# Beta added by GpSimd in the first-head passes, hop 1's first splits in the first group's normalization, and step 0's keys spread over twice as many pieces

## The chip, the core and the metric

The kernel runs on one core of a Trainium2 chip. The metric is the device time of one execution in microseconds (us); lower is better. The engines are called as in the profile: PE is TensorE (PEld its weight loads), DVE is VectorE, ACT is ScalarE, POOL is GpSimd and SP is SyncE, which only issues DMAs here. Each engine runs its own instructions in order; they meet through semaphores.

## The reference

Two graph layers on 4096 nodes of 256 features, each as x + layer(relu(layernorm(x))). Layer 0 is a graph attention with 4 heads over `adj`; layer 1 mixes two steps of a row-normalized adjacency (a "hop") with two steps of an attention that keeps the smallest set of entries whose weight reaches 0.9.

```python
h = relu(layernorm(x))
x = x + L0(h, adj)          # per head: e = leaky(src + dst), softmax where adj > 0, times h @ W
                            # then layernorm over the 256 outputs, * gamma + beta
h = relu(layernorm(x))
# L1(h, S=adj):
R = S + eye; R = R / R.sum(-1)
Z = 0; Xf = Xa = h
for n in range(2):
    A = top_p_attention(Xa, W1, W2, W3)   # softmax(q k^T), kept up to 0.9, renormalized
    Xf = R @ Xf
    Xa = A @ Xa
    Z = Z + Xf @ U1[n].T + Xa @ U2[n].T
x = x + layernorm(h + Z) * ln_g + ln_b
```

## The kernel before

The 4096 rows are 32 blocks of 128. `X` holds all of them in SBUF: first x, then the sum x + layer 0, then h of layer 1. Apart from scheduling hints, the order of the instructions on each engine is the order in which the code issues them (`manual_schedule`), within one such section. Between sections an engine may take up an instruction of a later section early if nothing holds it back and a buffer is free.

*Layer 0, prologue.* For each block: layer norm, product with W, exponentials, and a split of the values in three bf16 parts. POOL does a share of it: `third_part` (L275) and the copies into `ut` (L276).

*Layer 0, passes.* There are 16 passes k = (group ig of 8 blocks) x (head h), so that h = 0 in passes 0, 4, 8 and 12, the first-head passes. A pass goes over 16 pairs p of source blocks. For each pair, ACT (for two pairs of the pass DVE) makes the sign tile `g` (L366, L364), DVE makes two masks `m` from `g` and the edges `ax` (L372, L373), and PE multiplies (L392: 32 products into eight accumulator banks). Masks are issued two pairs ahead and have four buffers. Between passes `evacuate` takes the eight banks: an ACT copy with a scale (L406) and a DVE operation (L409) each, and in a first-head pass a DVE sum (L408). The next pass's first products need the first bank free.

The rest of a pass's work is put in the list `later`, of which one entry is done after each pair from p = 2 to p = 12: two for the heads, and behind the last head `closing`: four `stats`, eight `close`, four `relu`, 18 entries with the two. So a group's closing begins in the next group's first-head pass and ends one pass later; that of the last group (blocks 24 to 31) runs in hop 1.
- `stats` ends with `steps` on POOL (L141 to L144: an addition, a power, two products), which gives scale and bias.
- `close` of a block: ACT scales into `ob` (L441, two buffers), DVE multiplies with gamma (L442), POOL adds beta to the block's x (L443), DVE adds `ob` to it (L444), SP stores the row (L445), DVE takes the moments (L149, L150).
- After the eighth, `steps` again; `relu` then makes h of two blocks on ACT (L452).

POOL also copies one column of a mask (L485, "now") every sixth pair, to time the stores of edges to `adj_d` (L487) for the hops, and issues the edge loads of the next group.

*Hop 1* (`hops`) computes R @ X before its row scaling, transposed. It has 4 passes of 32 blocks; `order[n]` is the n-th (pass, block). For each n SP loads the edges `ar` (L572, four buffers, or `aru` for every fifth later), the block of X is split in a high and a low part `hl` (`split`: an ACT copy L579 and a DVE subtraction L580; five buffers, four blocks ahead), `own` adds the diagonal to one block in a group of 8 (DVE L589), and PE does eight products 128x512 (L602) into `mm` (a tile of two banks) and `acc`. The generator yields twice a block, 256 "pieces" in all, i = 0 to 255; a pass ends at i = 63, 127, 191. At its end `drained` copies the four accumulators to SBUF (L613, two by ACT and two by DVE, `acc` before `mm`), and the rows are turned and stored in the following pass.

The first 20 blocks (40 pieces) run beside the rest of the closing. From piece 40 on, each piece is followed by one piece of `fills` and one of `picks`, apart from those of block 30 (and for `picks` some more) in every pass:
- `fills` starts with `projections`, step 0's keys: eight groups of four blocks. Each transposes X (L752), copies it out (`xs`, L753), multiplies (L759) into a tile `pm` of the pool `mm`, copies that out (L761), and turns keys and queries into the other half of `pm` (L766), from where ACT and DVE split them into `kT` and `qT` (L768, L769). Then moments (L784), bounds (L806 and small tables), and for three blocks the logits (L707), their exponentials (L890) and four probes on ACT (L897).
- `picks` finds the threshold of those three blocks on DVE: two masked sums of half a row (L952), 18 maxima (L976), six rounds of a top-8 (L983, L985), small operations and two maskings of half a row (L952).

PSUM has two tiles `mm` (two banks each), of which the hop holds one for a whole pass, and two of `tp` and `acc`. What is left of `fills` and `picks` after the last piece is issued before the attention of step 0 starts. Then that step (to 1780 us), hop 2 and step 1 follow, in which the change touches nothing: `projections` has the same yields there, since n = 1.

The few lines that set the pace:

```python
                if 1 < p < PAIRS - 3 and later:
                    later.pop(0)()
...
                if (n == 0 or i > 10) and i // 2 % NB != NB - 2:
                    next(filling, None)
                    if i // 2 % NB < NB - 3 or i % (2 * NB) == 2 * NB - 1:
                        next(picking, None)
```

Of the kernel before, what the change touches and what calls it, by code (L numbers as in the profile page):

```python
# [11 lines left out]
F32 = mybir.dt.float32  # L12
F32R = mybir.dt.float32r
# [9 lines left out]
ALU = mybir.AluOpType  # L23
# [33 lines left out]
def gat_then_top_p_diffusion(  # L57
# [104 lines left out]
    with tc.tile_pool(name="l0", bufs=1) as l0, tc.tile_pool(name="l0s", bufs=2) as l0s, tc.tile_pool(name="l0o", bufs=1) as l0o:  # L162
# [175 lines left out]
        out_rows = {}  # L338
        later = []

        def sources(k):
# [54 lines left out]
        def evacuate(k):  # L396
# [27 lines left out]
            return [three, divided] + (closing(ig) if h == H - 1 else [])  # L424

        def closing(ig):
            o = out_rows[ig]
# [3 lines left out]
            def stats(i0):  # L431
                for i in range(i0, i0 + 2):
                    moments_of(mv[:, i, :], o[:, i, :])
                if i0 == G0 - 2:
                    scales.extend(steps(mv, G0, l0s))

            def close(i):
# [4 lines left out]
                nc.vector.tensor_mul(ob, ob, gamma_r)  # L442
                nc.gpsimd.tensor_tensor(xb, xb, beta_r, ALU.add)  # L443
                nc.vector.tensor_add(xb, xb, ob)  # L444
# [5 lines left out]
            def relu(i0):  # L450
                for b in range(ig * G0 + i0, ig * G0 + i0 + 2):
                    nc.scalar.activation(X[:, b, :], X[:, b, :], AF.Relu, scale=x_rs[:, b:b + 1], bias=x_nmr[:, b:b + 1])  # L452
            return [lambda i=i: stats(i) for i in range(0, G0, 2)] + [lambda i=i: close(i) for i in range(G0)] \
                + [lambda i=i: relu(i) for i in range(0, G0, 2)]
# [51 lines left out]
        with tc.manual_schedule(engines=every):  # L506
# [20 lines left out]
            for n, (k, p) in enumerate(todo):  # L527
# [10 lines left out]
                if n in rest:  # L538
                    rest[n]()
                if 1 < p < PAIRS - 3 and later:  # L540
                    later.pop(0)()
# [4 lines left out]
        ps1 = ctx.enter_context(tc.tile_pool(name="ps1b", bufs=2, space=PSUM))  # L546
        PASSES = NB // G0
        S = SimpleNamespace(spare=None)

        order = [(p, j) for p in range(PASSES) for j in range(NB)]  # L550

        def hop_of(hop):
            return SimpleNamespace(hop=hop, src={}, ar={}, hl={}, acc=None, begun=0, parted=0, owned=0)

        def source(A, n):
            if n in A.src or n >= len(order):
                return
            if A.hop == 0:
                A.src[n] = X[:, order[n][1], :]
            else:  # L560
                A.src[n] = S.rows.tile([P, D], F32, name="x1", bufs=3) if n % 5 < 3 else S.rows.tile([P, D], F32, name="xa")
                nc.sync.dma_start(A.src[n], xf_d[order[n][1]])

        def edge(A, n):
# [8 lines left out]
            A.ar[n] = ar  # L573

        def split(A, n):
            while A.parted < min(n, len(order)):
                src = A.src[A.parted]
                hl = rp.tile([P, 2, D], F32R, name="hl", bufs=5)
                nc.scalar.copy(hl[:, 0, :], src)  # L579
                nc.vector.tensor_tensor(hl[:, 1, :], src, hl[:, 0, :].bitcast(F32), ALU.subtract)  # L580
                A.hl[A.parted] = hl
                A.parted += 1

# [80 lines left out]

        first_hop = hops(hop_of(0))
        with tc.manual_schedule(engines=every | {ET.SP}):
# [50 lines left out]
    def waits(n):  # L717
        for i in range(n):
            yield

    def projections(cur, n, G):
# [25 lines left out]
        for g in range(NB // 4):  # L747
            xs = l1e.tile([P, 3, 4, P], F32, name="xs", tag="e1")
            for k in range(KC):
# [3 lines left out]
                nc.scalar.copy(xs[:, k], pt)  # L753
            yield from waits(1 + n)
            carried(xs, g, 0)
# [7 lines left out]
            carried(xs, g, 1)  # L763
            yield from waits(n)
            for i in range(4):
# [9 lines left out]
            carried(xs, g, 2)  # L775
            yield from waits(n)
            carried(xs, g, 3)
# [668 lines left out]
```

## Time and profile before

| | us |
|---|---|
| three runs | 2898.01, 2899.59, 2899.8 |
| median | 2899.59 |
| the profiled execution | 2899.5 |
| its span, first to last instruction | 2897.7 |
| mean granted clock of PE | 0.989 |

By stage, from the busy times of the profile's stretches:

| stretch (us from the start) | length | PE busy | DVE | ACT | POOL |
|---|---|---|---|---|---|
| 0 to 102.18, prologue | 102.2 | 65.6 | 78.4 | 65.8 | 79.2 |
| 102.18 to 810.44, layer 0's passes | 708.3 | 701.0 | 524.2 | 536.0 | 101.0 |
| 810.44 to 905, hop 1, pass 0 | 94.6 | 87.6 | 57.3 | 36.7 | 11.6 |
| 905 to 1010, hop 1 | 105.0 | 100.6 | 32.8 | 52.3 | 8.2 |
| 1010 to 1125, rest of hop 1 | 115.0 | 111.3 | 82.4 | 40.1 | 21.4 |
| 1165 to 1780, attention of step 0 | 615.0 | 614.2 | 540.8 | 489.1 | 196.6 |

How to read the profile: a line of the timeline gives start, length, engine, line of the kernel, operation and tiles, and in brackets the idle time of that engine before it with what released it. A line of waits gives the engine with its line, what it waited for, the sum in us, how often, and the longest. Products of PE overlap: two in flight make 0.39 us each a rate of 0.226.

### The profile page before, as it was taken

Reading aid. Unit: us, or ns where it says so; the run is one execution under the profiler, and the core shown is the slowest. Engines: PE = TensorE matmul, PEld = TensorE weight load, DVE = VectorE, ACT = ScalarE, POOL = GpSimd, SP = SyncE. Lnnn points to the kernel's source line nnn. Section 1 sums busy time; section 2 is a strip of 40 time slices with the busy share of each in tenths; the row PEclk is TensorE's granted clock in tenths of the full one; section 3 lists DMA queues with packets and bytes.
Section 4 is the critical chain, followed back from the end, with each engine's and each line's share of the span. In section 5 each row is a group of like instructions: output and inputs, shape, how many; then the busy total and the mean of one; then the engine's idle time right before and its main releaser. Section 6 shows DMA issues by size and latency. Waiting matters only on the chain. (4 is left out here: it accounts for less than half of the span.)

```text
span 2897.7 us, 51524 instructions
## 1 busy us (share of the span) xinstructions
PE 2814.0 (97%) x18777; PEld 2443.1 (84%) x18777; DVE 2171.2 (75%) x5069; ACT 1914.8 (66%) x3061; POOL 878.6 (30%) x1815
## 2 busy tenths in 40 slices
PE   6899999999999999999999999999999999999998
PEld 4799999999977778888888888767778888888887
DVE  7776877778654374888888889234474999999996
ACT  6786787868733634877788775222626777877782
POOL 6501211112010120233323331000204666666664
PEclk8899999999999999999999999999999999999999
DMA  7969577595454784000000000667992111111110
GB/s 177 217 247 223 187 227 195 211 224 187 177 189 158 238 298 164 20 20 26 20 20 20 26 20 19 231 197 236 313 352 68 31 31 38 34 31 31 39 31 25
DMA packets 190362, 376.48 MB, mean 130 GB/s; under 512 B 18192, under 2 KB 143120, under 8 KB 186000
## 3 DMA queue, kind: packets, MB, share of 16 engines
q1 hardware_dynamic: 146960, 275.12, 28.4%
q0 software_dynamic: 21504, 83.89, 12.2%
q10 hardware_dynamic: 21632, 14.05, 1.5%
q8 instruction: 152, 2.49, 0.3%
q14 instruction: 114, 0.93, 0.1%
HBM read 305.55 MB, written 113.57 MB: 145 GB/s over the span
## 5 line engine op out<-in xcount | busy, mean ns | idle before, releaser
L1075 PE MATMUL acc<-X,eT 128*128 128x256 f32 x4096 | 973.7, 383 | 3.3 <-ACT eT L1069 2.8
L1075 PEld LDWEIGHTS acc<-X,eT 128*128 128x128 f32 x4096 | 739.0, 190 | 111.4 <-ACT eT L1069 31.4
L392 PE MATMUL acc<-ut,m 128*128 128x195 bf16 (+1 forms) x8192 | 701.0, 247 | 8.2 <-DVE st L409 5.6
L392 PEld LDWEIGHTS <-m 128*128 128x128 fp8e4 x8192 | 696.4, 97 | 13.2 <-DVE st L409 4.7
L366 ACT ACTIVATE g<-sr,d_big 128x1024 uint8<-128x1024 f32 x444 | 467.7, 1139 | 2.6 <-DVE m L372 2.6
L890 ACT ACTIVATE e<-mm,nm 128x1024 f32<-128x1024 f32 x256 | 286.1, 1118 | 205.5 <-PE mm L707 204.1
L1069 ACT COPY eT<-tp 128x512 f32<-128x512 f32 x512 | 296.4, 580 | 89.7 <-PE tp L1067 89.6
L602 PE MATMUL mm<-ar,hl 128*128 128x512 f32 x844 | 341.8, 408 | 9.2 <-DMA ar<-adj_d 3.6
L976 DVE MAX8 cand<-big 128x8 f32<-128x228 f32 (+1 forms) x1152 | 348.3, 380 | 0.0
L958 DVE SCALAR_TENSOR_TENSOR big<-e,c 128x4096 f32<-128x4096 f32 x58 | 261.9, 4515 | 98.1 <-POOL c L943 58.8
L602 PE MATMUL acc<-ar,hl 128*128 128x512 f32 x844 | 328.3, 392 | 2.2 <-DVE ar L589 2.1
L914 POOL TENSOR_TENSOR sums<-sums 128x2 f32<-128x2 f32 x64 | 12.7, 198 | 1037.8 <-ACT void L897 1037.8
L1067 PE MATMUL tp<-ident,e 128*128 128x128 f32 x2048 | 306.1, 272 | 0.8 <-DVE e L1001 0.8
L1067 PEld LDWEIGHTS tp<-ident,e 128*128 128x128 f32 x2048 | 255.0, 140 | 60.4 <-PE acc L1085 1.2
L372 DVE TENSOR_TENSOR m<-g,ax 128x512 uint32<-128x512 uint32 x256 | 182.3, 712 | 115.5 <-PE acc L392 96.3
L897 ACT ACTIVATE void<-e,c1x 128x2048 int8<-128x2048 f32 x128 | 257.4, 2011 | 3.3 <-issue 2.5
L1001 DVE SCALAR_TENSOR_TENSOR e<-e,found 128x4096 f32<-128x4096 f32 x58 | 259.1, 4468 | 0.0
L897 ACT ACTIVATE void<-e,c 128x2048 int8<-128x2048 f32 x128 | 257.4, 2011 | 0.0
L707 PE MATMUL mm<-kT,qT 128*128 128x512 f32 x512 | 198.3, 468 | 3.6 <-ACT e L890 2.2
L602 PEld LDWEIGHTS mm<-ar,hl 128*128 128x128 f32 x844 | 158.8, 188 | 49.5 <-issue 9.2
L373 DVE TENSOR_TENSOR m<-m,ax 128x512 uint32<-128x512 uint32 x256 | 177.7, 694 | 26.0 <-DVE m L372 0.9
L602 PEld LDWEIGHTS acc<-ar,hl 128*128 128x128 f32 x844 | 158.8, 188 | 38.8 <-issue 4.1
(303 smaller groups left out, 3538.9 us busy)
## 6 DMA issues: line engine op xcount, KB each, us to landing
ar<-adj_d SPq DMA_DIRECT2D x211, 512.0 KB, 4.6
adj_d<-ax POOLq DMA_DIRECT2D x32, 2048.0 KB, 7.0
ut<-uv_d SPq DMA_DIRECT2D x60, 784.0 KB, 5.7
aru<-adj_d SPq DMA_DIRECT2D x45, 512.0 KB, 4.5
ax<-in_adj_t_dram POOLq DMA_DIRECT2D x32, 512.0 KB, 16.1
x<-xf_d SPq DMA_DIRECT2D x78, 128.0 KB, 4.9
xf<-xft_d SPq DMA_DIRECT2D x64, 128.0 KB, 2.2
sr<-s_d SPq DMA_DIRECT2D x15, 512.0 KB, 4.9
```

Of the source, the lines that this page charges most:

```text
L366: nc.scalar.activation(g[:, c, :], shared[k].sr, AF.Relu, scale=BIG, bias=d_big[:, h, j:j + 1])
L392: nc.tensor.matmul(shared[k].acc[i][:, t, :cols], m[t][:, c, ts(i, P)], shared[k].ut[j // QUARTER][:, j % QUARTER, t, :cols], start=(j == ...
L602: nc.tensor.matmul(A.acc[c][s], A.hl[m][:, t, ts(s, P)], A.ar[m][:, ts(c, 512)], start=(j == 0 and t == 0), stop=(j == NB - 1 and t == 1))
L707: nc.tensor.matmul(pm[:, h, :], q[t], kT[:, ds(h * (N // 2) + c * 512, 512)], start=(t == 0), stop=(t == 1))
L890: nc.scalar.activation(ev[:, :, c, :], r.pm[c], AF.Exp, bias=r.nm, accum_out=r.sums[:, c // 2, c % 2:c % 2 + 1])
L897: nc.scalar.activation(void, r.e[:, ts(h, N // 2)], (AF.Relu, AF.Sign)[i], bias=r.c1, scale=-1.0, accum_out=r.sums[:, h, 2 + i:3 + i])
L958: nc.vector.scalar_tensor_tensor(big, r.e, r.c3, r.e, ALU.is_le, ALU.mult, accum_out=r.low3)
L976: nc.vector.max(cand[:, s, :], big[:, edges[s]:edges[s + 1]])
L1001: nc.vector.scalar_tensor_tensor(r.e, r.e, r.t, r.e, ALU.is_ge, ALU.mult, accum_out=kept)
L1067: nc.tensor.transpose(pt[:, i, :], r.e[:, ts(4 * g + i, P)], ident)
L1069: nc.scalar.copy(eT, pt)
L1075: nc.tensor.matmul(r.acc[:, 0, :], eT[:, i, :], cur[:, j, :], start=(j == 0), stop=(j == NB - 1))
```

## The change

Three parts:
1. The POOL addition of beta leaves `close`. A list `lifted` of the 32 blocks is worked off in the first-head passes, one block after each pair from p = 3 to p = 14 while there are any, directly on `X`. So passes 0 and 4 take 12 each and pass 8 the last 8.
2. `source` and `split` move up in the code, unchanged, with `order`, `hop_of`, `S` and `PASSES`. The hop's state `hop1` is made before the passes, and the first group's `relu` of blocks 0 to 4 is followed by the blocks' split; `hops(hop1)` then finds five splits done.
3. In `projections`, at n = 0, a group takes six pieces for three: two in place of one ahead of the product, one more ahead of the turning of keys, one more at the end. At n = 1 the number stays.

```diff
@@ -337,6 +337,7 @@
         later = []
+        lifted = list(range(NB))
@@ -423,6 +424,34 @@
+        PASSES = NB // G0
+        S = SimpleNamespace(spare=None)
+
+        order = [(p, j) for p in range(PASSES) for j in range(NB)]
+
+        def hop_of(hop):
+            return SimpleNamespace(hop=hop, src={}, ar={}, hl={}, acc=None, begun=0, parted=0, owned=0)
+
+        def source(A, n):
+            if n in A.src or n >= len(order):
+                return
+            if A.hop == 0:
+                A.src[n] = X[:, order[n][1], :]
...
+        def split(A, n):
+            while A.parted < min(n, len(order)):
+                src = A.src[A.parted]
+                hl = rp.tile([P, 2, D], F32R, name="hl", bufs=5)
+                nc.scalar.copy(hl[:, 0, :], src)
+                nc.vector.tensor_tensor(hl[:, 1, :], src, hl[:, 0, :].bitcast(F32), ALU.subtract)
+                A.hl[A.parted] = hl
+                A.parted += 1
+
+        hop1 = hop_of(0)
+
         def closing(ig):
@@ -440,7 +469,6 @@
                 nc.vector.tensor_mul(ob, ob, gamma_r)
-                nc.gpsimd.tensor_tensor(xb, xb, beta_r, ALU.add)
                 nc.vector.tensor_add(xb, xb, ob)
@@ -450,6 +478,10 @@
                     nc.scalar.activation(X[:, b, :], X[:, b, :], AF.Relu, scale=x_rs[:, b:b + 1], bias=x_nmr[:, b:b + 1])
+                if ig == 0 and i0 < LOOK + 1:
+                    for b in range(i0, min(i0 + 2, LOOK + 1)):
+                        source(hop1, b)
+                        split(hop1, b + 1)
@@ -537,6 +569,9 @@
                     rest[n]()
+                if k % H == 0 and 2 < p < PAIRS - 1 and lifted:
+                    b = lifted.pop(0)
+                    nc.gpsimd.tensor_tensor(X[:, b, :], X[:, b, :], beta_r, ALU.add)
                 if 1 < p < PAIRS - 3 and later:
                     later.pop(0)()
...
-        first_hop = hops(hop_of(0))
+        first_hop = hops(hop1)
@@ -751,7 +760,7 @@
                 nc.scalar.copy(xs[:, k], pt)
-            yield from waits(1 + n)
+            yield from waits(2)
             carried(xs, g, 0)
@@ -761,7 +770,7 @@
             carried(xs, g, 1)
-            yield from waits(n)
+            yield
             for i in range(4):
@@ -773,7 +782,7 @@
             carried(xs, g, 2)
-            yield from waits(n)
+            yield
             carried(xs, g, 3)
             if n > 0:
                 yield
```

## The prediction

> **What bounds the kernel now.** I read the page first, then TensorE's waits, then the timeline of the engines around each gap.
>
> ```profile
> PE 2814.0 (97%) x18777; PEld 2443.1 (84%) x18777; DVE 2171.2 (75%) x5069; ACT 1914.8 (66%) x3061; POOL 878.6 (30%) x1815
> ```
>
> TensorE is busy 2814.0 of 2897.7 us. The change takes no TensorE work away, so it can only fill gaps: 83.7 us in all, of which the first 102 us (the prologue) hold 36.6, and the stages from 1780 us on, which are not touched, 24.2. Some 23 us of gaps are left to be had. The waits of TensorE that lie in the changed stretch (line, what was waited for: sum, times, longest):
>
> ```profile
> PE acc L392 <- DVE st L409: 5.6, 4, 1.6
> ...
> PE mm L602 <- DMA ar<-adj_d: 3.6, 4, 1.2
> ...
> PE mm L784 <- DVE qT L769: 1.9, 1, 1.9
> PE mm L759 <- DVE stage L613: 1.6, 1, 1.6
> ```
>
> Only four of the fifteen changes of pass in layer 0 cost TensorE anything. Its timeline there (start, length, idle before and releaser):
>
> ```profile
> 323.75 44.17 PE L392 MATMUL acc<-ut,m 128*128 128x195 bf16 x512 [1.33 <-DVE st L409]
> 369.53 50.69 PE L392 MATMUL acc<-ut,m 128*128 128x195 bf16 x594 [1.61 <-DVE st L409]
> ...
> 501.67 174.84 PE L392 MATMUL acc<-ut,m 128*128 128x195 bf16 x2048 [1.32 <-DVE st L409]
> 677.84 27.93 PE L392 MATMUL acc<-ut,m 128*128 128x195 bf16 x321 [1.33 <-DVE st L409]
> ```
>
> A pass has 512 products, so the 2048 from 501.67 on run through passes 9 to 12 with no gap: an evacuation costs nothing unless something delays it. What delays three of the four is in POOL's and DVE's timelines at 320 us (the same at 498 and 674):
>
> ```profile
> 320.52 1.42 POOL L443 TENSOR_TENSOR X<-X,beta_r 128x256 f32<-128x256 f32 x2
> ```
> ```profile
> 320.34 2.15 DVE L372 TENSOR_TENSOR m<-g,ax 128x512 uint32<-128x512 uint32 x1
> ```
>
> Two beta additions had queued on POOL behind the copy L485, which waited for a mask until 319.69; they run just then, and a mask that takes 0.69 us elsewhere takes 2.15, ahead of the evacuation on DVE. The fourth gap is ACT's:
>
> ```profile
> 366.34 1.62 ACT L579 CAST hl<-X 128x256 fp32r<-128x256 f32 x5
> 367.86 2.58 ACT L406 ACTIVATE st<-acc,e_c 128x195 f32<-128x195 f32 x8
> ```
>
> So hop 1's first five splits are not at the start of the hop: they already run in pass 5, just ahead of its evacuation. At hop 1's start, POOL and SP:
>
> ```profile
> 826.92 6.61 POOL L443 TENSOR_TENSOR X<-X,beta_r 128x256 f32<-128x256 f32 x8
> ```
> ```profile
> 829.54 0.34 SPq L445 DMA_DIRECT2D x_d<-X  x1
> 829.99 0.42 SPq L572 DMA_DIRECT2D ar<-adj_d  x1
> 832.28 0.34 SPq L445 DMA_DIRECT2D x_d<-X  x1
> 832.73 0.37 SPq L572 DMA_DIRECT2D ar<-adj_d  x1
> ```
>
> Each edge load `ar` queues on SP behind the store of a row that DVE has yet to finish. TensorE waits for `ar` at 833.76 (1.24), 836.63 (0.82) and 839.94 us (1.22). Last, the clock behind the change of pass in hop 1 (PE busy, other engines, granted clock, DMA):
>
> ```profile
> 905.00:906.00 1.00, 1.00 (x7) 1.00 (x7) 0.13 (x1) 0.00 (x0) 0.00 (x0) 0.50 0.06 16
> ```
>
> **What the Trainium skill says.** "SBUF — State Buffer", section "Who interferes with whom": a DVE instruction with two SBUF inputs and a GpSimd instruction that reads SBUF take one port pair in turn, and the loser blocks. The trace agrees (0.69 to 2.15 us beside 1.42 us of additions); in the run of five additions at 302.14 us DVE's two-input operations lose only 0.34 to 0.57 each. "TensorE: Matmul & The Clock Gate", section "What's actually happening": the clock falls to half after an idle window of about 3.4 us. The trace shows half clock from 905 to 908 us, though no single gap was that long: 0.97 and 1.64 us, four matmuls between.
>
> **Part 1, beta.** The 32 additions (0.72 to 0.77 us) leave `close` and go to p = 3 to 14 of passes 0 and 4 and p = 3 to 10 of pass 8. They wait for nothing, so POOL runs them as soon as its queue lets it; behind them stand the steps of the normalization and the stores `adj_d`, at most one addition later in passes 4 and 8, and those stores are read only in hop 1.
> - Changes of pass 8 to 9 and 12 to 13: no addition is left there; 1.32 + 1.33 = 2.65 gained. 4 to 5: the addition of p = 14 still follows L485, one in place of two: half of 1.33, 0.65 (0 to 1.33).
> - A wait of 0.17 for a mask in pass 13 (705.94 us) goes with the 1.0 us that `close` waits for POOL at 339 us (the same in each group).
> - Pass 0: POOL is in the prologue's last copies until 119.8 us, then some ten additions run in a row while DVE catches up. Pass 1 starts at 322.42 - 174.84 = 147.58 us (four passes without a gap), a pair of blocks takes 2.73, so the products of p = 8 and 10 start at 125.7 and 131.2; their masks are ready at 122.9 and 127.9, 2.8 and 3.3 us ahead. Taking turns, ten additions cost DVE ten times 0.34 to 0.72, 3.4 to 7.2 us, by p = 10 or 11: a stall of 0 to 3.9; I take 0.8, turn for turn.
> - Pass 4: POOL runs p = 8 to 13 in a row from 302 us, six where five were. The mask for p = 15 is ready at 319.02 us, its products start at 322.42 - 2.73 = 319.69: a margin of 0.67, of which the sixth takes 0.34 to 0.72. I take 0.3 (0 to 1).
> - Hop 1's start: DVE's five stretched operations lose 0.59, 0.35, 0.54, 0.36 and 0.57, 2.4 us. The stores and the `ar` loads behind them come up to 2.4 us earlier. The first two waits vanish, of the third a part stays, and the DMA share there is already 0.73 to 0.99: 2.3 of the 3.3 gained (0.5 to 3.3).
>
> **Part 2, splits.** Five ACT copies (1.5 us together) and five DVE subtractions (0.42) go from 366 to 345 us, between the `relu`s. ACT is busy without a gap from 343.69 to 367.86, so the move alone doesn't start the evacuation earlier. Two things do: the subtractions are out of DVE's way (it evacuates from 368.9 now), and the `relu`s start 1.0 to 1.5 us earlier, since `close` no longer waits for POOL. TensorE ends pass 5 at 367.92: 1.61 go to about 0.1, gain 1.5 (0.5 to 1.6). SP and POOL get nothing from it.
>
> **Part 3, keys.** Hop 1 yields 256 pieces, two for each block; keys start with piece 40. A group of four blocks takes 3 pieces before and 6 after, so all that follows comes 24 pieces later (21 where skipped pieces make up for it); no instruction is added. Groups 4 to 7 go past the change to pass 1, at piece 64.
> - The short waits inside groups (0.6 for `xs`, 0.2 for `qT`): 0.8 gained, since a further piece of four products (0.9 us) lies in between.
> - Change to pass 1: now 0.97 + 1.64 + 1.90 = 4.5. After it group 3 holds one of the two `mm` buffers over piece 64, so TensorE must wait for the other to drain: two DVE copies of 0.69 and signalling, 1.6. The moments' wait of 1.90 loses a piece of 0.9 and is 1.0. Gain 1.9 (0 to 3).
> - One gap of 1.6 has not dropped the clock elsewhere (1.90 before 912.11 did not). Products of L759 took 3.40 there against 2.31, L602's first 0.77 against 0.47: 1.4 gained (0 to 1.4).
> - Change to pass 2, piece 128: the first exponential of block 1 now falls on it, and its logits wait for the drain: 0.7 lost (0 to 1.5).
> - The three picks end later. By count, block 2's masking (2 x 2.35 us on DVE) falls behind the last piece. DVE is idle there between 1124.4 and 1132.3 us, so it is free; without that cover, 4.9.
> - TensorE lost 3.2 us to DVE and ACT at 1025 to 1036, with the picks. The same work comes 21 pieces later: no change (2 gained to 4 lost).
>
> **Sum.** Gains 2.65 + 0.65 + 0.17 + 2.3 + 1.5 + 0.8 + 1.9 + 1.4 = 11.4. Costs 0.8 + 0.3 + 0.7 = 1.8. Net 9.6, off the profiled execution's 2899.5 us (span 2897.7); that execution stands 0.1 below the median of the runs. Forecast 2890.0.
>
> **Rivals.**
> - *Only the beta part counts.* The change to pass 1 gains nothing and the clock stays low; piece 128 costs 1.5, the picks 1, and the additions of pass 0 stall TensorE for 3. Beta and splits gain 7.3 in the sum, so 7.3 + 0.8 - 1.5 - 1 - 3 - 0.3 = 2.3: 2897.2. For it: the buffer is held by count. Against: the gaps at 904 and 912 are there now, with less time to hide them.
> - *SP's loads are bound by DMA.* Rows and edges together are 640 KB for each block's 1.8 us of products, and the queues was at 349 GB/s at 840 us. Then hop 1's start gives nothing: 2892.3. For it: the share of 0.99; against: the first wait stands behind a late issue, at a share of 0.73.
> - *DVE saturates in the picks; slower.* A pick is 22.6 us of DVE work. In pieces 154 to 255 three picks less the last masking (62.9), 51 splits of 0.42 (21.4), 16 `own` additions of 0.28 (4.5) and two drains (2.7) come to 91.5 us, on 101 pieces of 0.906 (91.5) and some 4 us of logits and turned rows. If the backlog passes the four splits that run ahead (7.2 us), each further 2.35 us masking holds up TensorE as at 1025 us, 3.2 per 16 pieces, and over 101 pieces that is 20: 2890.0 + 20 = 2910. Against it: the same load fitted from 1002 to 1106 us before, with gaps.
>
> **How the numbers follow.** Forecast, a gain over 5.8 us (0.2%, about what a measurement can tell from no change), 0.54, with the start bound by DMA 0.12; beta only 0.22; saturation 0.12. Faster 0.66, same 0.22, slower 0.12. The bounds of the forecast alone, not all at once, reach from 2883 to 2895; with most of the second case, 2883 to 2898.
>
> **What would show it.** Right: no gaps near 499 and 675 us; a mask of at most 1.4 us near 320; ACT's evacuation near 366.5; no waits for `ar` in 826 to 842; one gap of about 1.6 at piece 64 and full clock behind it. Wrong: a wait for masks in 120 to 135 us, half clock after piece 64, waits for `hl` all through passes 2 and 3, or `big` drained late at the hop's end.

## The result and the profile after

| | before | after |
|---|---|---|
| median of six runs each, us | 2898.97 | 2884.53 |
| range, us | 2898.01 to 2902.43 | 2883.23 to 2890.51 |
| the profiled execution: its span, us | 2897.7 | 2881.5 |

The ratio of the times is 0.9952, with an interval of 0.9939 to 0.9965: the changed kernel is 14.4 us faster. The forecast was 9.6 us.

From here on the names of the lines are those of the changed kernel: L393 the products of layer 0 (L392 before), L373 and L374 the masks, L410 the evacuation on DVE, L574 the lifted additions of beta, L448 and L449 the splits, L473 and L590 the stores of rows and the edge loads on SP, L611 the products of the hop (L602 before), L768 those of the keys (L759 before). The row of busy times in the page of the changed kernel:

```profile
PE 2804.6 (97%) x18777; PEld 2442.7 (85%) x18777; DVE 2170.3 (75%) x5069; ACT 1916.2 (67%) x3061; POOL 882.0 (31%) x1815
```

The other engines do the same work as before. TensorE executes the same 18777 instructions and yet is busy 9.4 us less: not only gaps have gone, but also time in which it counted as busy while its products came more slowly. Apart from the clock, the forecast had looked for gaps alone.

TensorE's waits after (line, what was waited for: sum, times, longest):

```profile
PE acc L393 <- DVE m L373: 3.0, 2, 1.9
...
PE acc L393 <- DVE m L374: 1.6, 3, 0.6
PE mm L611 <- ACT ob L470: 1.6, 1, 1.6
PE mm L611 <- DVE stage L622: 1.4, 1, 1.4
...
PE tp L761 <- ACT stage L641: 1.0, 1, 1.0
...
PE mm L793 <- DVE qT L778: 1.0, 1, 1.0
PE mm L611 <- DMA ar<-adj_d: 0.9, 1, 0.9
...
PE acc L393 <- DVE st L410: 0.7, 1, 0.7
```

The evacuation's 5.6 us in four waits are down to 0.7 in one, and the waits for `qT` are 1.0 for 1.9. In return there are waits for masks (1.1 of L374's 1.6, and 1.06 of L373's 3.0; the rest of both lies near 102 us, as before) and one of a new kind, `tp` for `stage`. The waits at the hop's start are not gone: 1.63 us at 832.70, which is listed under `ob` although the hop's products do not read it, and 0.95 for `ar` at 842.97. The kernel before had 3.28 in three. TensorE's timeline in layer 0 shows where (start, length, idle before and releaser):

```profile
323.44 25.58 PE L393 MATMUL acc<-ut,m 128*128 128x195 bf16 x289 [0.71 <-DVE st L410]
349.56 2.81 PE L393 MATMUL acc<-ut,m 128*128 128x195 bf16 x31 [0.54 <-DVE m L374]
353.43 0.26 PE L393 MATMUL acc<-ut,m 128*128 128x195 bf16 x1 [1.06 <-DVE m L373]
354.22 365.97 PE L393 MATMUL acc<-ut,m 128*128 128x195 bf16 x4300 [0.54 <-DVE m L374]
```

The gaps near 499, 675 and 706 us are gone, and so is the one ahead of pass 6 near 369 us. The one ahead of pass 5 is 0.71 for 1.33. Three new ones stand inside pass 5, at 349 to 354 us. DVE's and POOL's timelines around the change from pass 4 to 5:

```profile
319.32 0.68 DVE L373 TENSOR_TENSOR m<-g,ax 128x512 uint32<-128x512 uint32 x1
320.11 0.69 DVE L374 TENSOR_TENSOR m<-m,ax 128x512 uint32<-128x512 uint32 x1
320.72 1.48 DVE L373 TENSOR_TENSOR m<-g,ax 128x512 uint32<-128x512 uint32 x1
```
```profile
302.46 4.98 POOL L574 TENSOR_TENSOR X<-X,beta_r 128x256 f32<-128x256 f32 x6
...
320.90 0.74 POOL L574 TENSOR_TENSOR X<-X,beta_r 128x256 f32<-128x256 f32 x1
```

One late addition makes one mask 1.48 us long, where two made it 2.15. Six additions in a row at 302 us cost TensorE nothing.

**How the stages were measured.** Two numbers can be read to about 0.1 us in every profile. The first is the start of the hop's first product. It has to be corrected for one thing: after the prologue TensorE's clock goes from half to full at a moment that differs by execution, between some 105.7 and 108.7 us, in all kernels alike. The products done from 100 to 112 us, counted in three windows of 4 us (79 to 98 in the executions here; 92 is taken as the norm), show by how much, at about 0.085 us each (the 32 products of a pair take 2.73). The second is the time from the hop's first product to a given piece, four products to a piece. Each row is one execution, the profiled one. In us:

| execution | hop 1 starts, corrected | pieces 0 to 40 | 40 to 255 |
|---|---|---|---|
| before, twice | 810.78, 810.71 | 41.17, 41.42 | 270.40, 270.26 |
| only beta | 805.81 | 39.29 | 268.23 |
| only splits | 812.71 | 42.74 | 267.93 |
| only keys | 810.79 | 42.42 | 261.47 |
| without splits | 805.96 | 39.42 | 261.43 |
| changed kernel, twice | 807.17, 807.25 | 39.54, 38.77 | 260.90, 260.53 |
| keys, four pieces | 807.14 | 40.15 | 263.92 |
| keys late | 807.13 | 38.54 | 265.26 |
| stores by POOL | 807.21 | 37.54 | 261.52 |
| moved | 803.33 | 40.31 | 261.12 |
| all three | 803.33 | 37.65 | 261.16 |
| stepped | 803.30 | 37.35 | 259.78 |

Kernels with the same layer 0 agree within 0.15 us in the first column, which shows that the correction holds. What follows the hop is 1773.0 to 1779.6 us in these executions, without an order by kernel: the totals of single executions scatter by that.

### The profile page after: what moved, and what is told of

It is laid out like the page before. It is cut to its first block, busy times and chain, and to the rows that moved or that the text cites. A ratio compares the mean times of both kernels' runs of the same rounds, so it can differ in the third digit from the quotient of the medians.

```text
span 2881.5 us, 51472 instructions
## 1 busy us (share of the span) xinstructions
PE 2804.6 (97%) x18777; PEld 2442.7 (85%) x18777; DVE 2170.3 (75%) x5069; ACT 1916.2 (67%) x3061; POOL 882.0 (31%) x1815
## 5 line engine op out<-in xcount | busy, mean ns | idle before, releaser
L393 PE MATMUL acc<-ut,m 128*128 128x195 bf16 (+1 forms) x8192 | 701.1, 247 | 5.4 <-DVE m L373 3.0
L393 PEld LDWEIGHTS <-m 128*128 128x128 fp8e4 x8192 | 698.0, 97 | 8.8 <-DVE m L373 4.2
L611 PE MATMUL mm<-ar,hl 128*128 128x512 f32 x844 | 341.2, 407 | 6.5 <-ACT ob L470 1.6
L611 PE MATMUL acc<-ar,hl 128*128 128x512 f32 x844 | 328.4, 392 | 0.2
L373 DVE TENSOR_TENSOR m<-g,ax 128x512 uint32<-128x512 uint32 x256 | 179.9, 703 | 106.7 <-PE acc L393 93.0
L374 DVE TENSOR_TENSOR m<-m,ax 128x512 uint32<-128x512 uint32 x256 | 180.5, 705 | 25.2
L611 PEld LDWEIGHTS mm<-ar,hl 128*128 128x128 f32 x844 | 158.6, 188 | 45.7 <-issue 5.8
L611 PEld LDWEIGHTS acc<-ar,hl 128*128 128x128 f32 x844 | 158.8, 188 | 36.6 <-issue 4.1
```

The costliest lines, as they stand in the source:

```text
L393: nc.tensor.matmul(shared[k].acc[i][:, t, :cols], m[t][:, c, ts(i, P)], shared[k].ut[j // QUARTER][:, j % QUARTER, t, :cols], start=(j == ...
L611: nc.tensor.matmul(A.acc[c][s], A.hl[m][:, t, ts(s, P)], A.ar[m][:, ts(c, 512)], start=(j == 0 and t == 0), stop=(j == NB - 1 and t == 1))
```

## The experiments

The first four take the parts of the change singly, on one chip, with 30 runs of the kernel before beside them (2900.68 us).

**Beta alone.** The kernel before with the list `lifted` and without the addition in `close`:

```diff
-                nc.gpsimd.tensor_tensor(xb, xb, beta_r, ALU.add)
...
+                if k % H == 0 and 2 < p < PAIRS - 1 and lifted:
+                    b = lifted.pop(0)
+                    nc.gpsimd.tensor_tensor(X[:, b, :], X[:, b, :], beta_r, ALU.add)
```

> The kernel before with the first part alone (beta lifted out of the closing). Theory A (from the two traces: the key pieces bring most): three gaps at changes of pass gone or halved, 2.65 + 0.6, the mask wait 0.17, hop 1's start 0.7, together about 4.0 us faster than before. Theory B (the sum on record): 5.8 gained less 1.1 lost, 4.7 faster. Theory C (beta is what counts): 8 or more faster. The change to pass 1 in hop 1 keeps its gaps of about 0.97, 1.64 and 1.90 us and its half clock under A and B.

Measured: 2893.22 us, ratio 0.9978 (0.9970 to 0.9986), 7.5 us faster by the medians, 4.1 to 8.7 by the interval: above theory A, between B and C, and the interval excludes neither of these two. The table has the parts: layer 0 ends 4.9 us earlier, the hop's first 40 pieces take 2.0 less. The gaps at the change to pass 1 stayed as theories A and B had it, but not the half clock, and that is another 1.5 us in pieces 64 to 72 (18.70 for 20.23). Theory A was too low in both of the first terms. In layer 0 the listed gaps shrank by only 3.3 us (5.76 to 2.47). The rest is in how a gap is read. These are the counts of one stretch with a gap of 1.32 us in it, in the kernel before, and then of the same 4 us without a gap in the kernel "moved" below (stretch and its length, then PE's busy time with its products, PEld, DVE, ACT, POOL, clock, DMA share, GB/s):

```profile
500.00:504.00 4.00, 2.68 (x29) 1.82 (x26) 3.90 (x18) 4.00 (x7) 0.00 (x0) 1.00 1.04 410
```
```profile
500.00:504.00 4.00, 4.00 (x49) 3.91 (x47) 3.93 (x8) 4.00 (x6) 0.00 (x0) 1.00 0.72 287
```

20 products are missing, 1.7 us at 0.085, where the gap is listed with 1.32. The timeline shows two reasons. A product is listed with 0.25 us although one starts every 0.085, so the idle time is counted from some 0.17 us too late. And behind the gap TensorE is "busy", but each bank has to wait for its own evacuation: the DVE operations come 0.39 us apart, where the four products of a bank take 0.34. Set against "moved", which has no gaps in layer 0, the kernel before loses 7.4 us there for 5.76 of listed gaps, and the changed kernel 3.9 for 2.85: 1.3 to 1.4 times the idle time.

**Keys alone.** The kernel before with the three waits of `projections` as changed:

```diff
-            yield from waits(1 + n)
+            yield from waits(2)
             carried(xs, g, 0)
...
-            yield from waits(n)
+            yield
...
-            yield from waits(n)
+            yield
```

> The kernel before with the third part alone (six pieces for a group of keys). Theory A: it takes most of the gain, 8 to 10 us faster than before; hop 1's start keeps its three waits for edges (3.3 us), and the four gaps at changes of pass in layer 0 stay. Theory B (the sum on record): 0.8 + 1.9 + 1.4 - 0.7 = 3.4 faster. Theory C: within 1 us of before, or slower.

Measured: 2892.62 us, ratio 0.9970 (0.9960 to 0.9980), 8.1 us faster by the medians; layer 0 is untouched (810.79 us), and the first 40 pieces are not shortened (42.42). Theory A holds, the sum on record does not for this part. Against the two kernels of old pace with full clock (268.23 and 267.93), pieces 40 to 255 take 6.6 us less, against the kernel before, which lost clock, 8.9.

**Splits alone.** The kernel before with the second part only:

```diff
                     nc.scalar.activation(X[:, b, :], X[:, b, :], AF.Relu, scale=x_rs[:, b:b + 1], bias=x_nmr[:, b:b + 1])
+                if ig == 0 and i0 < LOOK + 1:
+                    for b in range(i0, min(i0 + 2, LOOK + 1)):
+                        source(hop1, b)
+                        split(hop1, b + 1)
```

> The kernel before with the second part alone (five splits between the relus of the first group). Theory A: the gap of 1.6 us ahead of pass 6 goes, but waits for masks of about 2 us come up in pass 5 where the splits stand ahead of the signs on ACT: 0 to 1 us slower than before. Theory B (the sum on record): up to 1.5 faster, less whatever POOL's beta additions, which stay in the closing here, hold up.

Measured: 2902.38 us, ratio 1.0007 (0.9999 to 1.0016), 1.7 us slower by the medians, an interval that just takes in no change. Layer 0 ends 2.0 us later. Theory A's direction is confirmed by the profile, the record's sign is wrong.

**Without the splits.** The changed kernel less those four lines:

> The changed kernel without the second part: the splits of blocks 0 to 4 back at the hop's first pieces, beta and keys as changed. Theory A: pass 5 loses its waits for masks (2.1 us) and the gap of 1.6 ahead of pass 6 comes back: 0.5 us faster than the changed kernel, to 0.5 slower. Theory B: 1.5 us slower than the changed kernel, so 13 faster than before rather than 14.4.

Measured: 2884.85 us, ratio 0.9943 (0.9930 to 0.9957); the changed kernel has 0.9952, and the two intervals overlap. By the table layer 0 ends 1.2 to 1.3 us earlier without the splits. Pieces 40 to 255 take 0.5 to 0.9 more, but other kernels that have the splits in the relus lie as high (261.52), so that is scatter. The second part costs layer 0 1.2 us, and no gain stands against it. Beta alone and keys alone together give 15.5 us by the medians, and this kernel, which has both, 15.8: they add.

Why the splits cost is in ACT's timeline in pass 5 of the changed kernel:

```profile
345.94 1.07 ACT L480 ACTIVATE X<-X,x_nmr,x_rs 128x256 f32<-128x256 f32 x2
346.93 0.69 ACT L448 CAST hl<-X 128x256 fp32r<-128x256 f32 x2
347.53 2.18 ACT L367 ACTIVATE g<-sr,d_big 128x1024 uint8<-128x1024 f32 x2
...
351.89 14.65 ACT L367 ACTIVATE g<-sr,d_big 128x1024 uint8<-128x1024 f32 x14
368.30 2.80 ACT L407 ACTIVATE st<-acc,e_c 128x195 f32<-128x195 f32 x8 [1.76 <-PE acc L393]
```

A pair has 2.73 us. Two signs take 2.1 of it, a `relu` of two blocks 1.0, two splits 0.6: 3.7 in all, so ACT falls back by a microsecond with each pair that has all of these, and the signs, masks and products behind it with it. By the time of the evacuation it has caught up and is idle for 1.76 us. The count of products shows what it cost; the changed kernel first, then the kernel "moved" below, which has no splits in this pass:

```profile
340.00:350.00 10.00, 9.36 (x107) 8.74 (x105) 4.17 (x9) 7.75 (x13) 2.07 (x3) 1.00 0.71 259
350.00:360.00 10.00, 8.40 (x97) 8.01 (x96) 8.56 (x16) 10.00 (x13) 0.84 (x2) 1.00 0.14 54
```
```profile
340.00:350.00 10.00, 10.00 (x120) 10.00 (x118) 5.39 (x9) 8.19 (x13) 1.62 (x3) 1.00 0.67 246
350.00:360.00 10.00, 10.00 (x121) 10.00 (x119) 8.63 (x16) 10.00 (x11) 0.84 (x2) 1.00 0.59 229
```

204 products for 241: 37 fewer, 3.1 us, for 2.14 of listed gaps. Against that stands the gap ahead of pass 6 (1.75 listed in the kernel without splits).

The next four ask what the keys' gain is made of, and what bounds the hop's start (before: 2899.83 us).

**The kernel before, once more.**

> The kernel before, unchanged, profiled once more. The first profile shows half clock for 3 us behind the change to pass 1 of hop 1, and that stretch 1.5 us longer than in the two kernels that have only beta or only the splits changed, with gaps of the same lengths there. Theory A (the drop of the clock is the execution's, not the kernel's): full clock there in this execution, pieces 64 to 72 take 18.7 us for 20.2. Theory B (the kernel's gaps bring it): half clock again, 20.2 us.

Measured: 2900.26 us, one run. Pieces 64 to 72 take 20.18 us again, as theory B had it, but the half clock is not where it was. In the second execution the clock stays full behind 0.97 and 1.64 us and falls after the wait of 1.89 that ends at 910.87. Of five executions with such a group of gaps three lost clock, about 1.5 us each; only beta and only splits, with the same three gaps, did not. Of seven that have one gap of 1.4 us in its place and six pieces to a group none did: their pieces 64 to 72 all take 11.07 to 11.09.

What decides is the place of the gaps on a grid of 3.41 us, as the clock column of the profiles shows. Here are the stretches of that length around the changes of the clock, in the first profile of before, in this one, and in only splits (columns as above, the clock third from the end):

```profile
901.25:904.66 3.41, 1.56 (x7) 1.09 (x8) 3.31 (x7) 2.37 (x6) 0.00 (x0) 1.00 0.29 114
904.66:908.07 3.41, 3.41 (x17) 3.31 (x16) 0.83 (x3) 0.00 (x0) 0.00 (x0) 0.50 0.02 5
```
```profile
902.14:905.55 3.41, 1.77 (x12) 1.31 (x11) 3.24 (x7) 1.80 (x5) 0.00 (x0) 1.00 0.14 55
905.55:908.97 3.42, 3.42 (x22) 2.53 (x20) 0.96 (x2) 0.58 (x1) 0.00 (x0) 1.00 0.14 23
908.97:912.38 3.41, 1.52 (x19) 1.42 (x19) 2.70 (x5) 0.89 (x2) 0.00 (x0) 1.00 0.34 131
912.38:915.79 3.41, 3.41 (x21) 2.54 (x20) 0.55 (x2) 0.40 (x1) 0.00 (x0) 0.50 0.34 94
```
```profile
1030.02:1033.44 3.42, 1.65 (x7) 1.04 (x6) 3.25 (x15) 1.30 (x4) 2.84 (x8) 1.00 0.95 336
1033.44:1036.85 3.41, 3.24 (x14) 2.70 (x15) 3.27 (x11) 0.41 (x1) 3.05 (x6) 1.00 0.73 228
```

In each execution all changes of the clock lie whole multiples of 3.413 us apart: in the first profile at 105.94, 904.66 and 908.07 us (234 and 1 steps), in this one at 106.84, 912.38, 915.80, 1031.85 and 1035.26 (236, 1, 34 and 1). Where the grid lies differs by execution. In hop 1 the clock fell behind each stretch of the grid in which TensorE was idle for 1.85 us or more, five in all (1.85 in before, 1.89 and 1.92 in this execution, 2.24 in keys late, 2.58 in four pieces for a group), and behind none with 1.78 or less (only splits, above); each time it was full again one stretch later. So the gaps of 0.97 and 1.64 us together cost clock only where the grid puts enough of them in one stretch, and a single gap of 1.4 is too short for it by this count. Each theory holds half: the kernel's gaps make the loss possible, the execution decides. This execution lost clock a second time, behind a wait of 1.92 us at 1031.25; pieces 40 to 255 are not longer for it (270.26 for 270.40), since a wait of 0.66 that follows in the first execution is missing.

**Four pieces for a group.** Only the piece ahead of the product stays:

```diff
             carried(xs, g, 1)
-            yield
+            yield from waits(n)
...
             carried(xs, g, 2)
-            yield
+            yield from waits(n)
```

> The changed kernel with four pieces for a group of keys in place of six: only the further piece between the transposes and the product stays. Theory A (the distance between a copy and the product that reads it is what pays inside a group): the product of 16 takes some 2.0 us as with six pieces, the turning of keys still comes one piece behind its copy, so half or more of the 3 us of overlap is kept, but the keys now end at piece 72, across the change to pass 1: 0 to 3 us slower than the changed kernel. Theory B (it is only the pace, fewer key instructions for each piece): the gain goes with the number of pieces, a third of 6.7, so 4.5 us slower.

Measured: 2889.03 us, ratio 0.9962 (0.9948 to 0.9976). Pieces 40 to 255 take 263.92, 3.0 to 3.4 more than in the changed kernel's two profiles. That is between the theories, and it is not a matter of pace: one wait alone is longer than the difference. TensorE's, and what ACT had ahead of the split it waited for:

```profile
1019.94 0.47 PE L611 MATMUL mm<-ar,hl 128*128 128x512 f32 x1 [4.16 <-ACT hl L448]
```
```profile
1014.50 2.00 ACT L906 ACTIVATE void<-e,c1x 128x2048 int8<-128x2048 f32 x1
...
1016.79 2.00 ACT L906 ACTIVATE void<-e,c1x 128x2048 int8<-128x2048 f32 x1
```

Two probes with a split between them, in the reach of pieces whose products take 0.9 us each, use up the splits that ran ahead, and the clock falls behind it (0.66 from 1020 to 1025 us), which costs another 1.5 us or so. In the changed kernel the probes fall elsewhere, and the longest wait there is 0.72. Before those probes this kernel has no gap at all from piece 40 to 64 (38.90 us, all of them busy). So in this comparison the place of the later work decides more than the two further pieces of a group.

**Keys late.** The old three pieces for a group, and the 24 pieces that this saves put behind the groups:

```diff
...
+        if n == 0:
+            yield from waits(24)
         moments = rows.tile([2 * DA, DA + 1], F32, name="moments", tag="q_s", bufs=3)
```

> The changed kernel with the old pace of three pieces for a group, and 24 pieces of waiting between the eighth group and the moments, so that all that follows the groups comes where the changed kernel has it. Theory A (distance inside groups): groups lose their overlap again, product of 16 at 2.1 to 2.3 us, and the short waits come back: some 3.9 us slower than the changed kernel, less the 1.4 us wait at piece 64, which no group then meets: 2.5 slower. Theory C (what counts is what comes later: moments away from the change of pass, picks in a free place): as fast as the changed kernel or up to 1.4 faster.

Measured: 2887.80 us, ratio 0.9962 (0.9948 to 0.9976). Pieces 40 to 255 take 265.26, of which 1.5 is lost clock: 263.8. This splits the keys' gain in two, as far as single executions allow. From 268.1 (old pace, full clock: the mean of only beta and only splits) to 263.8 are 4.3 us that come from delay alone: moments, tables and picks that fall later. From 263.8 to 261.2 (the mean of the seven executions with six pieces and no other change to the keys) are 2.6 us from distance inside the groups, net of what the wider groups meet at the change to pass 1. That is the size of theory A, 2.5; theory C does not hold. The keys' products show it (busy us, mean ns, idle before and releasers), in turn before, only beta, this kernel and the changed one:

```profile
L759 PE MATMUL mm<-wkq,xs 128*128 128x128 f32 x128 | 18.6, 299 | 2.5 <-DVE stage L613 1.6 <-ACT xs L753 0.6 <-DVE qT L769 0.2
```
```profile
L762 PE MATMUL mm<-wkq,xs 128*128 128x128 f32 x128 | 17.2, 284 | 2.6 <-DVE stage L616 1.6 <-ACT xs L756 0.6 <-DVE qT L772 0.2
```
```profile
L768 PE MATMUL mm<-wkq,xs 128*128 128x128 f32 x128 | 18.8, 301 | 2.5 <-DVE stage L622 1.6 <-ACT xs L762 0.6
```
```profile
L768 PE MATMUL mm<-wkq,xs 128*128 128x128 f32 x128 | 15.6, 275 | 0.0
```

18.6 and 18.8 hold the lost clock, 17.2 does not. The idle time ahead of these products goes from 2.5 to nothing, and the same 128 products take 1.6 us less besides. The wait of 1.64 for the drain, which theory A had hoped away here, stayed: the eighth group still reaches past piece 64, because the pieces of block 30 carry no keys.

**Stores by POOL.** The changed kernel, with the rows of the last group stored by GpSimd:

```diff
-                nc.sync.dma_start(x1_d[b], xb)
+                (nc.gpsimd if ig == NB // G0 - 1 else nc.sync).dma_start(x1_d[b], xb)
```

> The changed kernel with the last group's stores of rows (x1) issued by GpSimd in place of SyncE, so that no edge load stands behind a store. Theory A (late issue): the waits of 1.63 and 0.95 us in the first 40 pieces go, those pieces take 37.7 us for 39.5. Theory B (the DMAs themselves are the limit there, at a share of 0.95 to 1.0): the waits stay within 0.5 us, 39 to 40 us.

Measured: one run of 2886.53 us; the first 40 pieces take 37.54 us, against 38.5 to 40.3 in the six kernels with beta lifted and the stores on SP. Theory A had said 37.7. The two kernels at the end that have this change as well take 37.65 and 37.35. SP's queue in the changed kernel, then in this one:

```profile
828.50 0.34 SPq L473 DMA_DIRECT2D x_d<-X  x1
828.93 0.38 SPq L590 DMA_DIRECT2D ar<-adj_d  x1
830.28 0.34 SPq L473 DMA_DIRECT2D x_d<-X  x1
830.72 0.72 SPq L590 DMA_DIRECT2D ar<-adj_d  x1
```
```profile
823.64 21.36 SPq L590 DMA_DIRECT2D ar<-adj_d  x12
```

A load no longer stands behind a store that waits for DVE, and each comes as soon as a buffer is free. Both waits of the changed kernel, 1.63 and 0.95 us, are gone, so the one listed under `ob` hung on the loads too. The DMA share was 0.94 to 1.02 in 827 to 843 us in this kernel (350 GB/s on average, 330 in the changed kernel), and yet the waits went. A share near 1 did not mean that the loads set the pace. The stores also go by another queue here; no run separates that from the order of issue.

The last four try what the experiments point to, beside the changed kernel on one chip (before: 2900.21 us).

**The changed kernel, once more.**

> The changed kernel, unchanged, on the same chip as the three that follow, so that they can be set beside it: 14 to 15 us faster than before, no half clock in hop 1, 39 to 40 us for its first 40 pieces.

Measured: 2886.78 us, ratio 0.9954 (0.9940 to 0.9968), 13.4 us faster by the medians, a little under what was expected, and the stages as in its first profile but for 0.8 us at the hop's start.

**Moved.** The splits go to pass 6, one after each of five pairs, and beta stops at p = 13:

```diff
-                if ig == 0 and i0 < LOOK + 1:
-                    for b in range(i0, min(i0 + 2, LOOK + 1)):
-                        source(hop1, b)
-                        split(hop1, b + 1)
...
-                if k % H == 0 and 2 < p < PAIRS - 1 and lifted:
+                if k == H + 2 and 2 < p < LOOK + 4:
+                    source(hop1, p - 3)
+                    split(hop1, p - 2)
+                if k % H == 0 and 2 < p < PAIRS - 2 and lifted:
```

> The changed kernel with the five splits in pass 6 (after the pairs p = 3 to 7, one each) in place of between the relus, and with beta added after p = 3 to 13 only, so that none follows p = 14 of pass 4. Theory A: the waits for masks in pass 5 (0.54 + 1.06 + 0.54 us) go, no gap comes back ahead of pass 6, and the gap of 0.71 ahead of pass 5 goes: 2.9 us faster than the changed kernel. Theory B (ACT and DVE are full in pass 5 whatever is added): the evacuation of pass 5 is late all the same, gain under 1 us.

Measured: 2882.77 us, ratio 0.9935 (0.9921 to 0.9948), 4.0 us faster than the changed kernel by the medians. Layer 0 ends 3.9 us earlier, for an expected 2.9: again the listed gaps (2.85) fall short of what they cost. Theory A holds. From pass 1 to pass 15 TensorE has no gap left; this is its line from 150 to 790 us:

```profile
149.84 640.35 PE L393 MATMUL acc<-ut,m 128*128 128x195 bf16 x7519
```

**All three.** With the last group's stores by POOL as well:

> As the one before, and the last group's stores of rows issued by GpSimd. Theory A: the gains add, 2.9 in layer 0 and 1.4 to 2.0 in hop 1, 4.3 to 4.9 us faster than the changed kernel, so about 19 faster than before. Theory B: what is gained ahead of hop 1 brings its loads closer together and is lost there again, under 3.

Measured: 2880.52 us, ratio 0.9931 (0.9918 to 0.9945), 6.3 us faster than the changed kernel beside it by the medians (4.3 to 4.9 expected) and 19.7 faster than before. The hop starts at 803.33, its first 40 pieces take 37.65: both gains are there in full. With the next one this is the fastest version found, and its interval lies below 0.9954, the ratio of the changed kernel on this chip (the two intervals overlap by 0.0005).

**Stepped.** The product of the fourth group held back past piece 64:

```diff
-            yield from waits(2)
+            yield from waits(7 if n == 0 and g == 3 else 2)
             carried(xs, g, 0)
```

> As the one before, and the product of the fourth group of keys held back by five pieces, past the change to pass 1, so that no group holds an mm buffer over piece 64. Theory A: the wait of 1.38 us for the drain at piece 64 goes, and the later steps move by five pieces at no cost: up to 1.4 us faster than the one before. Theory C: what comes later (moments, logits, picks) meets the change to pass 2 or the hop's end elsewhere, and 1 to 3 us are lost.

Measured: 2880.63 us, ratio 0.9929 (0.9914 to 0.9944): the same time as the one before. The wait of 1.38 us is gone, and pieces 40 to 255 take 1.4 us less, as theory A had it, but one execution's remainder is longer by more than that (1778.67 for 1775.77), and the median does not show a gain. Whether it is one stays open.

## Where the forecast held and where it failed

**Beta in layer 0** (recorded: 2.65 + 0.65 + 0.17 gained, 0.8 + 0.3 lost, net 2.4). The mechanism was right in each of its places: two gaps gone, one halved, the mask wait gone. The sizes were not: 4.9 us. The two costs did not come: pass 0's ten additions ran in a row, and pass 4 ended no later than before in only beta (322.55 for 322.76, corrected); the sixth addition in pass 4 cost nothing. And each gap was priced at its idle time, where the products missing in one such stretch make 1.7 us of a gap of 1.32. One sign on record did not come: the mask near 320 us took 1.48 us, not at most 1.4.

**Hop 1's start** (2.3). Measured 1.9 to 2.5: the mean of the first 40 pieces is 41.94 us in the four executions without the lifted beta (41.30 in the two of the kernel before) and 39.43 in the seven executions with it and with stores on SP. The size was right, but the waits did not go as the record had it: TensorE still waits for 1.2 to 2.6 us in these pieces in the seven executions, for 3.3 to 4.7 in the four, and in the changed kernel 1.63 of it falls at 832.70 us, where the record had no wait. The rival that held SP's loads to be bound by DMA has fallen with the stores on POOL, which gave two microseconds more.

**Splits** (1.5 gained). This is the step that failed in its sign: 1.2 us lost in layer 0. The record saw ACT "busy without a gap" from 343.69 to 367.86 and priced a move inside that stretch at nothing. It looked at the end of the stretch and not at what stands behind the five copies at their new place: signs, then masks, then products. The `relu`s did start 1.4 us earlier (342.25 for 343.69), and the gap ahead of pass 6 went as forecast; but three others came, and ACT's evacuation starts at 368.30, for 366.5 on record and 367.86 before, because it now waits for the late products.

**Keys, 40 to 255** (0.8 + 1.9 + 1.4 - 0.7 + 0 for the picks = 3.4). Measured 6.9 us at full clock on both sides (268.1 to 261.2), and some 1.5 more in executions that lose clock before.
- The clock (1.4) was sized rightly, but the loss comes in three executions of five with those gaps, as the grid falls; the step missing on record is that the idle time in one stretch of it counts, not a single gap.
- The change to pass 1 (1.9 gained) was too hopeful. TensorE's timeline of the changed kernel there:

```profile
882.36 0.50 PE L611 MATMUL mm<-ar,hl 128*128 128x512 f32 x1 [1.38 <-DVE stage L622]
897.53 0.66 PE L633 MATMUL tp<-ident,stage 128*128 128x128 f32 x4 [0.31 <-ACT xs L762]
```
```profile
906.00 0.66 PE L761 MATMUL tp<-ident,X 128*128 128x128 f32 x4 [1.01 <-ACT stage L641]
924.95 1.12 PE L793 MATMUL mm<-e 128*64 128x65 f32 x16 [0.97 <-DVE qT L778]
```

  1.38 for the drain and 0.97 for the moments are within 0.3 us of the 1.6 and 1.0 on record. Not foreseen were 0.31 and 1.01: the rows of the finished pass are turned through the same two `tp` tiles as the keys, which now run beside them. 3.67 for 4.51: 0.8 gained.
- Piece 128 (0.7 lost): 0.37 + 0.31 us at that place, right; but one of the three waits of 0.36 to 0.39 that the logits had before is gone, so some 0.3 are lost on balance.
- What made up for it was not on record. A wait of 1.40 us for `own` at 951 us, beside the tables, does not come up any more; at the picks waits of 1.93, 0.66 and 0.57 us became 0.72 and 0.51, where the record had no change; and products inside the groups overlap better, 1.6 us in the keys' own row.

**The tail and the third rival.** No cost behind the last piece: the first product after it waits 0.47 us, for 0.46 before. DVE did not saturate in the picks: between 979 us and the hop's end TensorE waits only for 0.51 and 0.72 us. *Only the beta part counts* is refuted by the kernel with keys alone.

So the total was low by 4.8 us; the result lies in the bounds of the forecast, 2883 to 2895, near their lower end. Layer 0 comes out at 3.6 gained for 3.9 forecast (2.4 + 1.5), but out of two errors that cancel; hop 1's start is right in size; the keys were underrated by more than half, mostly in the parts that the record set at nothing.

## What to carry to other kernels

Price a stall by the products missing in a window around it, not by the idle time listed ahead of one instruction. On an engine that works in order, a moved instruction costs whoever stands behind it at the new place: compare its length with what that engine has free for each step there (here the signs left 0.6 us of each pair's 2.73, and the `relu`s already took more), not with the whole stretch. Keep a store that waits for a slow engine out of the queue that issues the loads. And where gaps cost clock, profile more than one execution: the same gaps can cost it or not.

## What the runs showed of the hardware

- The clock of TensorE changed only on a grid of 3.41 us, whose place differs by execution. It fell to half behind each stretch of the grid with 1.85 us or more of idle time in hop 1 and behind none with 1.78 or less. Over all 14 executions, from 112 us to the end, it never fell behind less than 1.8 us in one stretch and always behind more than 1.95. "TensorE: Matmul & The Clock Gate", section "What's actually happening", in the Trainium skill has an idle window of about 3.4 us. The length agrees, but here somewhat over half of it idle was enough: the only single gap in hop 1 that was longer than 3.4 is the one of 4.16 us, and its two stretches held 1.58 (no fall) and 2.58 (fall).
- One GpSimd addition of 0.74 us beside a DVE mask of 0.68 made it 1.48, two made it 2.15: DVE lost about what GpSimd took. This agrees with the turn-taking in "SBUF — State Buffer", section "Who interferes with whom". Ten additions beside a full DVE took 1.05 us each (10.47 us from 120.11) for 0.74, and TensorE did not notice.
- With a DMA share of 0.94 to 1.02 in 827 to 843 us, the loads still were not what bounded TensorE: taking the stores out of their queue gained 2 us without a byte less.
